# Layer 0 attention: the row maxima turned by VectorE and carried by DMA into a spare row of the queries, and the causal mask as four 32-row products per head

## The chip, the cores and the metric

The kernel runs on one core of one Trainium2 chip. The metric is device time in microseconds, the median of three runs. All times below are microseconds unless ns is written. The engines are named as in the profile: PE is TensorE, DVE is VectorE, ACT is ScalarE, POOL is GpSimd, SP is SyncE, which issues most DMAs.

## The reference, cut to what matters

The kernel computes two pre-norm transformer layers on x of 4 x 512 x 256. Layer 0 is a causal attention of 16 heads of 16, and a mixture of 8 experts; layer 1 is an attention over the four sequences at equal positions, and a gated MLP with 4-bit weights. The change lies in layer 0's attention:

```python
q, k, v = (qkv[0], qkv[1], qkv[2])
att = jnp.einsum('bhqd,bhkd->bhqk', q, k) / math.sqrt(HEAD_DIM)
causal = jnp.triu(jnp.ones((s, s), dtype=bool), k=1)
att = jnp.where(causal[None, None, :, :], jnp.float32(-1000000000.0), att)
att = jax.nn.softmax(att, axis=-1)
out = jnp.einsum('bhqk,bhkd->bhqd', att, v)
```

Layer 1's attention is touched in one operand only: a 0/1 pattern with which its scores are multiplied, so that each token sees only the four tokens of its own position.

## The kernel before

**Tiling.** The 512 positions are cut into four blocks j of 128. The 16 heads form four groups g of four; head h of a group lives in the partitions 32h to 32h+31. The tile `qk` (L463) holds, for each group, six slots of [4 sequences x 128 positions]: slots 0 to 3 are the keys of the four blocks, slots 4 and 5 the queries of the current block (slot 4 + j mod 2). A head's 32 partitions are used so: rows 4 to 19 hold the 16 dimensions, which `project` (L534) sends there by DMA from a staging tile, eight DMAs per half. Rows 0 to 3 of the keys hold a constant pattern, one in row g of group g, which POOL writes beforehand from `mask32` (`blank`, L470, and L481); rows 0 to 3 of the queries begin as zeros (L485, L506).

**Batches.** The attention runs in 44 batches n (L649): for every block j and sequence s, four, two, one or one groups at a time. A batch has five steps:

- `greatest` (L660): the scores, queries by keys, 16 x (groups / 4) matmuls on 32 rows each, into four PSUM tiles, one per head of the group. The pool `ps_sc` has five such banks.
- `mask` (L675): onto the last block of each tile, one bf16 matmul with the identity `ident_h` adds the upper triangle `later`, filled with -1e30. Then DVE takes the maximum over the keys, four TENSOR_REDUCEs at L687, into one of two tiles `maxes`.
- `shift` (L692): PE transposes `maxes` into PSUM (L697), so that each group's maxima stand in one of the rows 0 to 3 of the head's partitions; DVE subtracts the result from the queries (L700). The constant row of the keys then takes the maximum off all scores.
- `powers` (L706): the same scores a second time, keys by queries, so that keys lie on the partitions, now less the maximum (L716); ACT takes the exponential (L725), POOL zeroes what lies above the diagonal (L735).
- `mixed` (L743): the product with the values (L752), in the one bank of `ps_mm`, which the transposed maxima of `shift` use too.

**Order.** PE, DVE, POOL and ACT run in the order in which the program is written (`manual_schedule`, L73); SP does so too until batch 3 (L76, L899), and by priorities afterwards. The loop at L863 issues for batch n: `greatest(n + 1)`, `shift(n)`, `mask(n + 1)`, a filling, `mixed(n - 1)`, `powers(n)`, a second filling. A filling (`fill`, L149) takes pieces of the mixture of experts (L234, the router's and the experts' products, with the DVE work behind them), of projections of the next block and of layer norms, until a budget for PE or DVE is spent. The four routers' and experts' weight loads per batch (L891, n below 4) and the blanks of the later blocks (L893) follow.

**Start.** POOL first builds the identity, then copies and zeroes parts of `qk` (L481, L485), makes `ident_h` and `later`, and then computes two reciprocal roots for the first layer norm (L634). `blanks(xn)` (L500) zeroes `maxes` and the second query slot behind it.

**Elsewhere.** `mask8` (L95, L850) is `fold8` repeated four times; layer 1 multiplies by it at L1044.

## Time and profile before

| | us |
|---|---|
| median of three runs | 1166.89 (1166.68 to 1167.87) |
| span of the profiled execution | 1164.9 |
| PE busy | 1144.1 (98%) |
| DVE busy | 812.4 (70%) |
| ACT busy | 481.9 (41%) |
| POOL busy | 108.2 (9%) |

The profile is of one execution. Its span runs from the first to the last instruction; a run's time is some 2 more. The granted clock of TensorE is 0.999 on the mean. A group of instructions is shown as line, engine, operation, output <- input, shapes and count, then the busy time and the mean of one in ns, then the idle time of the engine before them and what ended it. An f32 matmul shows as two records, each with a weight load (PEld) of its own.

The lines that belong to the steps above, besides those that the prediction shows:

```profile
L716 PE MATMUL s<-qk 32*128 32x128 f32 x1280 | 54.5, 287 | 0.5
L697 PE MATMUL mxT<-ident,mx 128*128 128x128 f32 x44 | 14.4, 327 | 0.0
L681 PE MATMUL s<-later,ident_h 128*128 128x128 bf16 x128 | 12.4, 219 | 0.0
L700 DVE TENSOR_TENSOR qk<-qk,mxT 128x128 f32<-128x128 f32 x32 | 9.0, 282 | 15.0 <-PE mxT L697 14.9
L476 POOL COPY qk<-mask 128x512 f32<-128x512 f32 x12 | 7.5, 644 | 0.0
```

Durations of PE records overlap: a record of 219 ns starts 55 ns behind the one before it. What a piece adds to the time is read from the chain of waits in order of time, where each piece begins when the one before it ends.

Layer 0's attention takes the stretch from about 22 to 385. Busy time in parts of it:

| stretch | length | PE | DVE | ACT | POOL |
|---|---|---|---|---|---|
| 62 to 120 | 58.0 | 56.99 | 38.54 | 26.21 | 15.08 |
| 120 to 168 | 48.0 | 47.99 | 42.73 | 26.51 | 11.97 |
| 198 to 242 | 44.0 | 44.00 | 39.90 | 26.11 | 9.51 |
| 242 to 283 | 41.0 | 40.80 | 39.98 | 23.44 | 7.22 |
| 283 to 325 | 42.0 | 41.83 | 36.80 | 26.10 | 5.97 |
| 325 to 362 | 37.0 | 35.85 | 34.74 | 20.80 | 4.55 |

### The profile page before, as it was taken

The page shows a single profiled execution, that of the slowest core. Times are in us where ns is not written, and L with a number is a line of the kernel's source. Part 1 is how long each engine was busy: PE and PEld are TensorE (multiplying, and loading weights), DVE is VectorE, ACT ScalarE, POOL GpSimd, SP SyncE. Part 2 cuts the span into 40 slices and gives each one's busy share as a digit, 9 for nine tenths or more (in the row PEclk, how much of TensorE's full clock was granted, in tenths as well). Part 3 has the DMA queues.
Part 4 walks back from the last instruction along what each step waited for, and adds up shares of the span by engine and source line. Part 5 has one row for each costly group of instructions (what it writes and reads, how often), then busy time and mean ns, then how long its engine had stood idle before and what let it go on. Part 6 is the DMA issues. An engine that isn't in the chain of part 4 may idle for free.

```text
span 1164.9 us, 18575 instructions
## 1 busy us (share of the span) xinstructions
PE 1144.1 (98%) x7182; PEld 662.6 (57%) x7182; DVE 812.4 (70%) x1788; ACT 481.9 (41%) x1095; POOL 108.2 (9%) x153
## 2 busy tenths in 40 slices
PE   9999999999998999999999999999999999999998
PEld 5666555555554445555555555566544475484487
DVE  6675899999988844868663776687699835716710
ACT  1444555555655542444443444444344313303300
POOL 8322221212112000000000000000000000000000
PEclk9999999999999999999999999999999999999999
DMA  4440100000000500000000001110110000000000
GB/s 130 118 120 2 27 12 1 2 2 2 2 2 1 181 1 1 1 1 0 1 1 1 1 1 46 33 51 19 27 46 1 0 1 19 0 1 19 1 19 18
DMA packets 21527, 26.46 MB, mean 23 GB/s; under 512 B 5160, under 2 KB 15144, under 8 KB 21440
## 3 DMA queue, kind: packets, MB, share of 16 engines
q1 hardware_dynamic: 20624, 24.10, 7.6%
q10 hardware_dynamic: 816, 1.18, 0.4%
q8 instruction: 56, 0.92, 0.3%
q14 instruction: 31, 0.25, 0.1%
HBM read 18.97 MB, written 2.10 MB: 18 GB/s over the span
## 4 chain that ended last, share of the span: by engine, by line
PE 82%; DVE 13%; issue 2%; ACT 1%; POOL 1%; SPq 0%; DMA 0%; POOLq 0%; DVEq 0%; ACTq 0%
PE qk_ps L1019 11%; PE y L1266 9%; PE o L1110 9%; PE g L948 9%; PE u L948 9%; PE lg_ps L234 8%; PE eo L234 7%; PE s L668 3%; PE s L716 3%; DVE mx L687 3%; PE av L752 2%; PE v_ps L1001 2%; PE qk_ps L539 2%; PE a L1090 1%; PE s L1032 1%
## 5 line engine op out<-in xcount | busy, mean ns | idle before, releaser
L1019 PE MATMUL qk_ps<-xT,wqkv 128*128 128x512 f32 x320 | 148.9, 599 | 2.3 <-ACT part L323 1.2
L234 PE MATMUL lg_ps<-rw,xT 128*128 128x512 f32 x256 | 122.5, 601 | 1.4 <-ACT xT L986 0.3
L234 PE MATMUL eo<-ew,xT 128*128 128x512 f32 x256 | 121.5, 600 | 0.8 <-ACT lg L297 0.5
L1110 PE MATMUL o<-wpj,oT 128*128 128x256 f32 x512 | 119.1, 382 | 0.0
L1266 PE MATMUL y<-wd,it 128*128 128x256 f32 x512 | 111.8, 379 | 0.0
L1110 PEld LDWEIGHTS o<-wpj,oT 128*128 128x128 f32 x512 | 95.9, 190 | 27.5 <-issue 14.3
L1266 PEld LDWEIGHTS y<-wd,it 128*128 128x128 f32 x512 | 97.0, 190 | 15.0 <-issue 2.2
L687 DVE TENSOR_REDUCE mx<-s 128x1 f32<-128x384 f32 (+3 forms) x176 | 100.5, 633 | 0.2 <-PE s L681 0.2
L1019 PEld LDWEIGHTS qk_ps<-xT,wqkv 128*128 128x128 f32 x320 | 59.1, 190 | 71.4 <-issue 57.4
L725 ACT ACTIVATE pt<-s 128x512 f32<-128x512 f32 (+1 forms) x176 | 84.1, 565 | 35.9 <-PE s L716 35.9
L948 PE MATMUL g<-xT,wgu 128*128 128x512 f32 x192 | 90.4, 593 | 0.0
L948 PE MATMUL u<-xT,wgu 128*128 128x512 f32 x192 | 90.2, 592 | 0.0
L323 ACT ACTIVATE part<-eo,c 128x256 f32<-128x256 f32 x128 | 53.6, 471 | 84.7 <-PE eo L234 74.8
L735 POOL TENSOR_SCALAR_AFFINE_SELECT pt<-pt 128x256 f32<-128x256 f32 (+2 forms) x88 | 62.4, 716 | 246.9 <-ACT pt L725 246.7
L1244 ACT ACTIVATE th<-sq 128x512 f32<-128x512 f32 x64 | 40.3, 630 | 87.8 <-DVE sq L1243 87.8
L234 PEld LDWEIGHTS lg_ps<-rw,xT 128*128 128x128 f32 x256 | 46.1, 190 | 46.1 <-issue 37.3
L234 PEld LDWEIGHTS eo<-ew,xT 128*128 128x128 f32 x256 | 46.1, 190 | 45.7 <-issue 38.3
L222 DVE TENSOR_TENSOR xres<-xres,y 128x256 f32<-128x256 f32 x16 | 6.7, 421 | 92.5 <-PE y L1266 92.5
L297 ACT COPY lg<-lg_ps 128x512 f32<-128x512 f32 x64 | 37.6, 588 | 73.5 <-PE lg_ps L234 73.5
L185 POOL TENSOR_TENSOR ln_rs<-rs_v,minus_half 128x4 f32<-128x4 f32 x15 | 16.6, 1103 | 552.2 <-DVE rs_v L184 440.0
L1245 DVE SCALAR_TENSOR_TENSOR th<-th,g 128x512 f32<-128x512 f32 x63 | 43.2, 686 | 29.3 <-ACT th L1244 29.2
L948 PEld LDWEIGHTS u<-xT,wgu 128*128 128x128 f32 x192 | 36.5, 190 | 45.9 <-issue 44.7
(240 smaller groups left out, 1782.5 us busy)
## 6 DMA issues: line engine op xcount, KB each, us to landing
qk<-stage SPq DMA_DIRECT2D x56, 64.0 KB, 2.4
wqkv<-in_w_qkv SPq DMA_DIRECT2D x8, 320.0 KB, 6.4
rw<-in_router_w SPq DMA_DIRECT2D x8, 256.0 KB, 4.8
ew<-in_expert_w SPq DMA_DIRECT2D x8, 256.0 KB, 5.5
wpj<-in_w_proj SPq DMA_DIRECT2D x1, 2048.0 KB, 12.5
out<-xres SPq DMA_DIRECT2D x4, 512.0 KB, 2.7
xres<-in_x SPq DMA_DIRECT2D x3, 512.0 KB, 4.8
dq_wgu<-in_gate_w SPq DMA_DIRECT2D x8, 128.0 KB, 2.4
```

Source lines behind the costliest of these rows:

```text
L234: nc.tensor.matmul(ps, lhsT=xT[:, hc, (g % 4) * P : (g % 4 + 1) * P], rhs=w[:, hc, 2 * pair : 2 * pair + 2, :].rearrange("p e o -> p (e o) ...
L297: nc.scalar.copy(lg[:, 2 * pair : 2 * pair + 2, :].rearrange("p e o -> p (e o)"), ps)
L323: nc.scalar.mul(part[:, e % 4], ps[:, i], c[:, e : e + 1])
L687: nc.vector.tensor_reduce(maxes[n % 2][:, h, gs[0] : gs[0] + nb], ps[:, : nb * nk].rearrange("p (b k) -> p b k", b=nb), AX.X, ALU.max,)
L725: nc.scalar.activation(pt[:, i, : nb * nk], tiles[2 * pair + i][:, : nb * nk], AF.Exp, scale=0.25)
L735: nc.gpsimd.affine_select(out=last, in_=last, compare_op=ALU.is_ge, fill=0.0, base=0, pattern=pattern, channel_multiplier=-1,)
L948: nc.tensor.matmul(ps, lhsT=wgu[:, w, half, jj, par * P : (par + 1) * P], rhs=xT[:, half, :], start=half == 0, stop=half == 1,)
L1019: nc.tensor.matmul(ps, lhsT=wqkv[:, hc, kv, h, :], rhs=xT[:, hc, :], start=hc == 0, stop=hc == 1,)
L1110: nc.tensor.matmul(ys[t // 2][:, t % 2], lhsT=state["o"][:, h, t * P : (t + 1) * P], rhs=wpj[:, HPK * kv + h, :], start=kv == 0 and h == 0 ...
L1244: nc.scalar.activation(th, sq, AF.Tanh, scale=0.7978845608028654)
L1245: nc.vector.scalar_tensor_tensor(th, th, 1.0, gp, ALU.add, ALU.mult)
L1266: nc.tensor.matmul(ps, lhsT=it[:, c // 2, c % 2, t * P : (t + 1) * P], rhs=wd[:, c // 2, c % 2, :], start=c == 0, stop=c == 2 * NJ - 1,)
```

## The change

The 16 dimensions of a head now stand in rows 0 to 15 of its 32 partitions, and row 16 is a spare row. In the keys it holds -1, which four DMAs write at the start from a tile `minus`; in the queries it takes the maximum of each query. The first scores use rows 0 to 15, the second rows 0 to 16.

The maxima are laid down in one tile [128 queries, group, 32], heads in the first four columns. DVE turns them in blocks of 32 x 32 (`mT`, one buffer), so that partition 32a + h holds head h's maxima of the queries 32a to 32a+31. Four DMAs from SP, one for each a, write them into row 16 of the four heads. PE's transpose, its place in `ps_mm` and DVE's subtraction go.

`shift(n + 1)` now follows `mask(n + 1)`, where `shift(n)` stood between `greatest(n + 1)` and `mask(n + 1)`; `shift(0)` is issued before the loop.

The mask's one product of 128 rows per tile becomes four of 32 rows. The rows c of a diagonal block, 32 queries at a time, have their own triangle in the columns from 32c on; `pick` chooses the 32 output rows, and head h's product reads the partitions 32h to 32h+31. The loop over c is outside, that over the heads inside.

The pattern rows of the keys, the zeroed queries, `ident_h` and `mask8` are not needed any more; layer 1 multiplies by `fold8` with another view of the same elements. POOL's blanks of later blocks shrink to those of the values, and the conditions that waited for the others go.

```diff
     fold8 = const.tile([P, 8], F32, name="fold8")
-    mask8 = const.tile([P, NS, 8], F32, name="mask8")
...
         qk = w0.tile([P, 4, NBLK + 2, NS, P], F32, name="qk")
-        maxes = [w0.tile([P, 4, 32], F32, name=f"mx{i}") for i in range(2)]
+        maxes = w0.tile([P, 4, 32], F32, name="mx")
+        nc.vector.memset(maxes, 0.0)
         va = w0.tile([P, NBLK * NS * NH0 * 17 + 15], F32, name="va")
...
         wo = w0.tile([P, 2, HID], F32, name="wo")
-        def blank(j, i):
-            if i == 4:
-                to = va.shape[1] if j == NBLK - 1 else (j + 1) * per_block
-                nc.gpsimd.memset(va[:, j * per_block : to], 1.0)
-            else:
-                nc.gpsimd.tensor_copy(
-                    qk[:, i, j].rearrange("p s q -> p (s q)"),
-                    mask32[:, i : i + 1].to_broadcast([P, 512]),
-                )
-        nc.gpsimd.tensor_copy(
-            qk[:, :, 0].rearrange("p g s q -> p g (s q)"),
-            mask32[:, :4].unsqueeze(2).to_broadcast([P, 4, 512]),
-        )
-        nc.gpsimd.memset(qk[:, :, NBLK].rearrange("p g s q -> p g (s q)"), 0.0)
-        ident_h = w0.tile([P, P], BF16, name="ident_h")
-        nc.gpsimd.tensor_copy(ident_h, ident)
+        def blank(j):
+            to = va.shape[1] if j == NBLK - 1 else (j + 1) * per_block
+            nc.gpsimd.memset(va[:, j * per_block : to], 1.0)
+        minus = b1.tile([P, HID], F32, tag="w1", name="minus")
+        nc.gpsimd.memset(minus, -1.0)
+        for g in range(4):
+            nc.sync.dma_start(
+                out=qk[16:P:32, g, :NBLK].rearrange("p j s q -> p (j s q)").rearrange(
+                    "p (i k) -> p i k", k=HID
+                ),
+                in_=minus[0:4].unsqueeze(1).to_broadcast([4, 8, HID]),
+            )
+        pick = w0.tile([P, 224], BF16, name="pick")
+        nc.gpsimd.memset(pick, 0.0)
+        nc.gpsimd.tensor_copy(pick[:, 96:P], mask32)
         later = w0.tile([P, P], BF16, name="later")
         nc.gpsimd.memset(later, 0.0)
-        nc.gpsimd.affine_select(
-            out=later, in_=later, compare_op=ALU.is_ge, fill=NEG,
-            base=0, pattern=[[-1, P]], channel_multiplier=1,
-        )
+        for i in range(4):
+            nc.gpsimd.affine_select(
+                out=later[32 * i : 32 * i + 32], in_=later[32 * i : 32 * i + 32],
+                compare_op=ALU.is_ge, fill=NEG, base=0, pattern=[[-1, P]], channel_multiplier=1,
+            )
         bs = b1.tile([P, 2, 512], F32, tag="hi4", name="bs")
...
         bp = rows[:, 8:].rearrange("p i q -> p (i q)")
-        def blanks(xn):
-            after = b2.tile([P, 1], F32, tag="rs_v", name="after")
-            nc.gpsimd.tensor_copy(after, xn[:, 3, 0:1])
-            for i in range(2):
-                nc.gpsimd.memset(maxes[i], 0.0)
-            nc.gpsimd.memset(qk[:, :, NBLK + 1].rearrange("p g s q -> p g (s q)"), 0.0)
         def split_biases():
...
                     eng.dma_start(
-                        out=qk[h + 4 : h + 20, 2 * half + r // 4, j : to + 1 : to - j].rearrange(
+                        out=qk[h : h + 16, 2 * half + r // 4, j : to + 1 : to - j].rearrange(
                             "p i s q -> p i (s q)"
...
                 for s in (0, 2):
-                    yield need("PE", 1.75, 1, cond=lambda: blanked > 5 * j - 10)
+                    yield need("PE", 1.75, 1, cond=lambda: blanked > j - 2)
                     values(j, xT, s)
...
                         "PE", 1.75, 0 if half or i else 1,
-                        cond=lambda: j < 2 or done >= 8 * j - 12 and blanked >= 5 * j - 5,
+                        cond=lambda: j < 2 or done >= 8 * j - 12,
                     )
...
                 for h in range(4):
-                    r = slice(32 * h, 32 * h + 32)
+                    r = slice(32 * h, 32 * h + 16)
                     nc.tensor.matmul(
...
                         lhsT=queries(j, g)[r, s], rhs=qk[r, g, : j + 1, s, :],
...
             j, s, gs = batches[n]
...
             tiles = open_scores.pop(n)
-            for ps in tiles:
-                nc.tensor.matmul(
-                    ps[:, : nb * nk].rearrange("p (b k) -> p b k", b=nb)[:, :, j * P :],
-                    lhsT=ident_h, rhs=later.unsqueeze(1).to_broadcast([P, nb, P]),
-                    start=False, stop=True,
-                )
+            for c in range(4):
+                for h, ps in enumerate(tiles):
+                    r = slice(32 * h, 32 * h + 32)
+                    left_of = P - 32 * c
+                    nc.tensor.matmul(
+                        ps[:, : nb * nk].rearrange("p (b k) -> p b k", b=nb)[
+                            :, :, j * P + 32 * c :
+                        ],
+                        lhsT=pick[r, 96 - 32 * c : 224 - 32 * c],
+                        rhs=later[r, :left_of].unsqueeze(1).to_broadcast([32, nb, left_of]),
+                        start=False, stop=c == 3,
+                    )
             for h, ps in enumerate(tiles):
                 nc.vector.tensor_reduce(
-                    maxes[n % 2][:, h, gs[0] : gs[0] + nb],
+                    maxes[:, :nb, h],
                     ps[:, : nb * nk].rearrange("p (b k) -> p b k", b=nb), AX.X, ALU.max,
...
         def shift(n):
             j, s, gs = batches[n]
-            ps = ps_mm.tile([P, P], F32, tag="mm", name=f"mxT_{n}")
-            nc.tensor.transpose(ps, maxes[n % 2].rearrange("p h g -> p (h g)"), ident)
             g, nb = gs[0], len(gs)
-            q = qk[:, g : g + nb, 4 + j % 2, s, :]
-            nc.vector.tensor_tensor(
-                q, q, ps.unsqueeze(1).to_broadcast([P, nb, P]), ALU.subtract
-            )
+            mT = a1.tile([P, 4, 32], F32, tag="mT", name=f"mT_{n}")
+            nc.vector.transpose(
+                mT[:, :nb].rearrange("p b q -> p (b q)"),
+                maxes[:, :nb].rearrange("p b h -> p (b h)"),
+            )
+            for a in range(4):
+                nc.sync.dma_start(
+                    out=qk[16:P:32, g : g + nb, 4 + j % 2, s, 32 * a : 32 * a + 32],
+                    in_=mT[32 * a : 32 * a + 4, :nb],
+                )
         powers_of = {}
...
                     for h in range(4):
-                        r = slice(32 * h, 32 * h + 32)
+                        r = slice(32 * h, 32 * h + 17)
                         nc.tensor.matmul(
...
                             lhsT=qk[r, g, c, s, :], rhs=queries(j, g)[r, s],
...
         xn = normed_by_twos()
-        blanks(xn)
         xT = a1.tile([P, 2, NS, P], F32, tag="xT0", name="xT0_0")
...
         normed.clear()
-        for i in range(5):
-            blank(1, i)
+        blank(1)
         split_biases()
...
         )
-        nc.vector.tensor_copy(mask8, fold8.unsqueeze(1).to_broadcast([P, NS, 8]))
         xT = unused("xT0_1", "p (h s q) -> p h s q", h=2, s=NS)
...
         greatest(0)
         mask(0)
+        shift(0)
         inputs = {1: Stream(projections(1, xT))}
...
                 if n + 1 < NBT:
                     greatest(n + 1)
-                shift(n)
                 if n + 1 < NBT:
                     mask(n + 1)
+                    shift(n + 1)
             fill(PE=(2.0, 2.0, 1.8, 1.6)[j], DVE=2.6)
...
                     loaded[n // 2, (4 * n % 8 + i) // 2] = slot
-            for _ in range(1 + (n < 2) if blanked < 10 else 0):
-                blank(2 + blanked // 5, (blanked + 4) % 5)
+            if blanked < 2:
+                blank(2 + blanked)
                 blanked += 1
...
         ps_y = l1.enter_context(tc.tile_pool(name="l1_y", bufs=1, space=PSUM))
-        seen = mask8.rearrange("p s b -> p (s b)").unsqueeze(1).to_broadcast([P, 16, 32])
+        seen = fold8.unsqueeze(1).to_broadcast([P, 64, 8])
         state = {}
...
             )
-            nc.vector.tensor_tensor(sm, sm, seen, ALU.mult)
+            by_8 = sm.rearrange("p i (s b) -> p (i s) b", b=8)
+            nc.vector.tensor_tensor(by_8, by_8, seen, ALU.mult)
             sc = c1.tile([P, 16, 4], F32, tag="sc", name=f"sc{p}")
...
                 sc.rearrange("p i s -> p (i s)"),
-                sm.rearrange("p i (s b) -> p (i s) b", b=8), AX.X, ALU.add,
+                by_8, AX.X, ALU.add,
             )
```

## The prediction

> **What bounds the kernel now.** I read the page's chain of waits first, then the same chain in order of time inside layer 0, then the timeline there, and last the groups of instructions and the DMA issues. All numbers are microseconds unless marked ns.

> ```profile
> PE 82%; DVE 13%; issue 2%; ACT 1%; POOL 1%; SPq 0%; DMA 0%; POOLq 0%; DVEq 0%; ACTq 0%
> PE qk_ps L1019 11%; PE y L1266 9%; PE o L1110 9%; PE g L948 9%; PE u L948 9%; PE lg_ps L234 8%; PE eo L234 7%; PE s L668 3%; PE s L716 3%; DVE mx L687 3%; PE av L752 2%; PE v_ps L1001 2%; PE qk_ps L539 2%; PE a L1090 1%; PE s L1032 1%
> ```

> TensorE sets the end; the change touches only lines worth a few per cent each, and VectorE (DVE) is the one rival. The chain in order of time shows one batch bounded by TensorE:

> ```profile
> 203.26 0.86 PE s L668 x8
> 204.12 0.26 PE mxT L697
> 204.38 0.22 PE s L681 x4
> 204.60 1.77 PE eo L234 x4
> 206.38 0.79 PE av L752 x24
> 207.17 0.88 PE s L716 x24
> 208.05 1.91 PE eo L234 x4
> ```

> Columns: start, length, what. First scores, transpose of the maxima, mask, filler, mixing, second scores, filler. The same four records of filler cost 1.77 behind the mask, which uses the whole array, and 1.91 behind the second scores, which use 32-row quarters: leaving quarters costs 0.14. In j=3 (four blocks of keys) some batches are bounded by DVE instead:

> ```profile
> 249.61 0.20 DVE qk L700
> 249.81 2.40 DVE mx L687 x4
> 252.20 0.08 DVE sums L436
> ```

> Summed over 24 to 365, DVE holds about a quarter of the chain. I count 13 of the 44 batches as DVE-bound, all of one head group; 31 as TensorE-bound: 19 of one group (j=2, 3), 8 of two (j=1), 4 of four (j=0).

> **TensorE: mask and transpose.** Gone for a batch of one, two, four groups are the transpose, 0.26, and the mask, 0.22, 0.44, 0.86 (four products of 128 columns per group, so 0.055 per 128 columns in bf16). Added are 16 products on 32 rows. No row has bf16 products on 32 rows. The nearest are L716 and L668: L716 takes 0.88 for 24 records (above) and 1.10 for 32 (j=3), so 8 records of 128 f32 columns add 0.22, that is 0.11 for each four. A full-array f32 record of 512 columns takes 0.43 (1.72 over four), so 128 columns 0.107: the four quarters run wholly beside each other. In that case a head's columns alone count, 128+96+64+32 = 320 per group, and 320 at 0.055 per 128 is 0.14, 0.28, 0.55. Then the filler follows quarters and not the whole array: +0.14. Per batch: 0.14+0.14-0.26-0.22 = -0.20; 0.28+0.14-0.26-0.44 = -0.28; 0.55+0.14-0.26-0.86 = -0.43. The other bound is that the quarters run one after another: 1280 columns, 0.55, 1.10, 2.20, which makes +0.21, +0.54, +1.22. I take the first, since L716 and L668 have the same rows, banks and order. That the maxima fall due a little later (all four tiles close together at the end of the mask) is met by the transpose that no longer stands ahead of it.

> The trace's own starts inside one four of L716 lie 6.6 ns apart (275.649, 275.656, 275.663, 275.669). [...]

> On the path I count 19 x 0.20 = 3.8, of which I keep three quarters, 2.9, because DVE is busy 39.9 of 44.0 in 198 to 242 and 36.8 of 42.0 in 283 to 325 and will take back some; 7 x 0.28 = 2.0 (one batch of j=1 lies beside the wait for layer norm at 81 to 92); 3 x 0.43 = 1.3 (batch 0's mask ends in a wait for DVE). Together -6.2; from -10.4 (all 44 in full) to +13.2 (31 batches, one after another).

> **VectorE.** Gone are 44 subtractions L700, 0.28, 0.42, 0.69 busy and 0.20 on the chain; added are 44 transposes of 32, 64, 128 columns.

> ```profile
> L687 DVE TENSOR_REDUCE mx<-s 128x1 f32<-128x512 f32 x64 | 39.6, 681 | 0.0
> L687 DVE TENSOR_REDUCE mx<-s 128x1 f32<-128x384 f32 x64 | 31.1, 548 | 0.0
> L1041 DVE STREAM_TRANSPOSE sm<-s 128x512 f32<-128x512 f32 x16 | 11.4, 715 | 28.1 <-PE s L1032 28.1
> ```

> 128 columns are worth 133 ns between the first two; 480 columns fewer than L1041 leave 715 - 499 = 216 ns. So 0.20 goes and 0.2 comes: 0 in the 13 DVE-bound batches, between -0.1 and +0.2 each (-1.3 to +2.6). In the TensorE-bound ones DVE's idle tenth hides it; without that cover it would cost the same 0.2. The transpose waits in addition until the four DMAs of the batch before have read `mT` (one buffer); behind it stand DVE's filler and the next four maxima, for which the second scores wait (five banks). Layer 1's multiplication by `fold8` instead of `mask8` keeps 128x512 elements; L1044 and L1070 take 692 ns each with either operand, so 0. L850 (1.41 at 22.1) falls away beside TensorE's scores: 0.

> **SyncE and the new wait.** Four DMAs per batch are new, 176 in all, and the second scores wait for them where they waited for L700. Behind those scores in TensorE's order stand the filler and the next mixing, and ACT's exponentials wait for them. The nearest rows:

> ```profile
> qk<-stage SPq DMA_DIRECT2D x56, 64.0 KB, 2.4
> dq_sgu<-in_gate_s SPq DMA_DIRECT2D x64, 16.0 KB, 1.7
> 33.20 5.61 SPq L549 DMA_DIRECT2D qk<-stage  x8
> 242.35 2.48 DVE L687 TENSOR_REDUCE mx<-s 128x1 f32<-128x512 f32 x4
> 251.26 1.55 PE L716 MATMUL s<-qk 32*128 32x128 f32 x32
> ```

> Three issues of L549 go before the fourth starts: 3 x 0.64; with the transpose, 0.2, the fourth's issue and landing, 2.4, and a handing over or two, about 4.6 to 5.2. The batch shown (28) has its maxima at 244.83 and its scores at 251.26: 6.4 of room, because `shift` is moved ahead by a whole step, past one filling, a mixing and another batch's scores. Read so for all 44, the room is 5.1 at batch 0, 5.6 at the next smallest, 7.5 at the median. `mT` comes free likewise: the maxima of neighbours end 6.1 or more apart but for batch 1 (4.0). I take +0.5 for batches 0 and 1. In SP's queue the move passes stage DMAs (eight per half, 5.1) and the router and expert loads. The stage sets of j=2 start at 67.9 and 76.5, of j=3 at 134.2 and 141.7; the maxima of batches 5 and 6 end at 67.7 and 76.25, of 13 and 14 at 134.3 and 141.3, so each set would come just behind a shift and be done before the next one: 0, and up to 2 each if the order is the other way.

> **Start and GpSimd.** Up to the first root POOL loses these copies and gains small memsets and three selects of 0.29:

> ```profile
> 1.92 1.88 POOL qk L481
> 3.80 1.74 POOL qk L485
> 6.28 1.50 POOL ln_rs L634 x2
> ```

> About 4.4 of POOL work becomes some 2.3, so the roots wait for their variances alone (5.57 and 6.53; statistics that run beside POOL's copies take 0.78 where others take 0.39). The second root would end at 7.3 or earlier instead of 7.78: -0.7, between 0 and -1.5. The four DMAs of `minus` put 1.7 ahead of the second load of x, which is used only at 10.67: 0. Later blanks (12 x 0.64 and a memset of 1.8) lie on an engine busy 9%: 0.

> **Sum.** -6.2 + 0 + 0.5 - 0.7 = -6.4, against the profiled execution's span of 1164.9: 1158.5. The median of the runs is 1166.89, 2.0 more than that span; with the same 2.0, 1160.5. I say 1161.

> **Rivals.** (1) The DMAs come late, slower. For: eight stage DMAs on the two queues have landed after 3.8, the longest issue took 1.44. Against: the rooms above. It decides where transpose, issues and landing exceed 6.7: summed over the batches' rooms, that is 7.0 of delay, which eats the gain. At 7.2 it is 14.3, so 1166.9 - 6.4 + 14.3 = 1174.8; 0.17. (2) The quarters' bf16 products run one after another: +13.2 + 0.5 - 0.7, 1180; halfway to it, 1170. Against it is L716; 0.11. (3) No change: 16 weight loads per batch set the mask's pace (L681's load takes 0.098; four rounds are 0.39, so +0.05, -0.17, -0.43 per batch), or DVE takes back all of the rest: some 1165.5; 0.19. What speaks for it is DVE's nine tenths.

> **How the numbers follow.** Faster 0.53, these rivals 0.17, 0.11 and 0.19. From -10.4 the low end is 1156; the high end reaches into (1) and (2) to 1172, with some 0.12 above and 0.07 below. The forecast's own range is 1156 to 1164.5. About 0.2%, 2.3, is what a measurement of this kernel can tell from no change: faster 0.53, within it 0.19, slower 0.28.

> **What would show it.** In the chain of the changed kernel, no mxT; L681's successor at 0.14 to 0.2 for one group; the filler behind it at 1.91; transposes of about 0.22 with no wait for a DMA; second scores waiting for maxima and not for DMAs; the second root done by 7.3. It is wrong if the mask of one group takes 0.4 or more, if waits of TensorE or DVE for a `qk<-mT` DMA add up to over 5, or if DVE's part of the chain grows by what TensorE's loses.

## The result, and the profile after

The changed kernel took 1174.74 us (four runs, 1173.9 to 1177.43), the kernel before, run beside it, 1167.06: ratio 1.007, 95% interval 1.0056 to 1.0085. It is slower, by some 8 us, and outside the range that was forecast. The profiled execution's span is 1172.6 against 1164.9.

The page's parts on busy time, on the granted clock in 40 slices, and on the chain of waits:

```profile
PE 1148.4 (98%) x7666; PEld 668.7 (57%) x7666; DVE 808.4 (69%) x1788; ACT 481.2 (41%) x1095; POOL 96.0 (8%) x140
...
PEclk8999997999999999999999999999999999999999
...
PE 81%; DVE 13%; ACT 1%; issue 1%; DMA 1%; SPq 1%; POOL 0%; DVEq 0%; POOLq 0%; ACTq 0%
```

TensorE still sets the end and DVE's part of the chain has not grown. New in the chain are SP's queue and a DMA, 1% each. TensorE is busy 4.3 longer than before, although it has less to do; the clock line, 9 in every slice before, shows an 8 and a 7.

One batch in layer 0, the chain in order of time (start, length, what), as for the kernel before:

```profile
212.90 0.86 PE s L660 x8
213.76 0.14 PE s L676 x15
213.90 1.91 PE eo L233 x4
215.82 0.79 PE av L753 x24
216.61 0.88 PE s L717 x24
```

Here the change does what was forecast. Scores, mask and filler took 0.86 + 0.26 + 0.22 + 1.77 = 3.11 and take 0.86 + 0.14 + 1.91 = 2.91. Where the clock stays full, the second scores of neighbouring batches come 0.20 closer together in j=2 (batches 12 to 15: 6.22, 6.02, 5.82, 5.61 behind the same scores of the kernel before) and 0.26 closer in j=1 (batches 2 to 6, between whose second scores stand the masks of batches 4 to 7: 6.56 down to 5.54).

But the attention begins late. The chain in order of time at the start:

```profile
3.78 0.68 SPq L478
4.46 0.04 issue
4.50 1.57 SPq L478
6.07 0.04 issue
6.12 7.06 DMA xres<-in_x
13.17 0.02 issue
13.20 0.44 DVE ln_st L179
...
16.82 3.15 DVE xn L193 x4
19.97 0.60 DVE stage L535
20.57 0.04 issue
20.62 6.29 PE v_ps L553 x16
```

SP's four DMAs of -1 (L478) hold up the second load of x; the layer norm of block 1 waits for it, DVE comes late to a copy that `v_ps` of block 0 needs, and `v_ps` then takes 6.29 where it took 3.72. The first scores begin at 28.27 instead of 22.43. TensorE's timeline of the kernel before, then the first scores of the changed kernel (start, length, line, output <- input, count):

```profile
17.34 3.72 PE L561 MATMUL v_ps<-wp,xT 128*128 128x256 f32 x16 [0.60 <-DVE stage L543]
22.43 2.08 PE L668 MATMUL s<-qk 32*128 32x128 f32 x32
```

```profile
28.27 1.17 PE L660 MATMUL s<-qk 16*128 16x128 f32 x32
```

And the gain does not last. Busy time in stretches of the changed kernel, then of the kernel before (stretch, its length, busy time and count of PE, PEld, DVE, ACT, POOL, then the granted clock, DMA's share, GB/s):

```profile
20.00:40.00 20.00, 18.30 (x161) 12.49 (x161) 9.62 (x17) 1.17 (x2) 8.40 (x16) 0.77 0.24 54
160.00:200.00 40.00, 39.13 (x405) 21.95 (x405) 34.67 (x89) 20.15 (x57) 8.92 (x11) 0.87 0.03 5
240.00:270.00 30.00, 30.00 (x342) 15.60 (x344) 28.28 (x67) 17.68 (x51) 5.30 (x8) 0.94 0.01 1
```

```profile
20.00:40.00 20.00, 19.42 (x199) 13.26 (x202) 12.26 (x21) 4.22 (x8) 11.92 (x20) 1.00 0.38 74
160.00:200.00 40.00, 38.59 (x387) 21.11 (x390) 37.75 (x96) 22.33 (x62) 9.19 (x12) 1.00 0.01 1
240.00:270.00 30.00, 29.80 (x325) 16.94 (x324) 27.94 (x61) 16.66 (x47) 4.13 (x6) 1.00 0.01 1
```

The trace's record of the granted clock says where: it halves at 19.0, 32.7, 97.5, 176.0, 196.5, 257.9 and 353.5, for 3.41 or 6.83 each time, 34.1 in all. Two of these stretches (columns as above):

```profile
19.01:25.83 6.82, 5.21 (x12) 4.21 (x13) 2.84 (x6) 0.00 (x0) 6.39 (x8) 0.50 0.40 68
176.02:182.85 6.83, 6.83 (x56) 4.01 (x54) 5.60 (x17) 3.11 (x7) 0.93 (x2) 0.50 0.02 3
```

In the kernel before the clock never halves between 6 and 1150. Batch 16 stands 5.54 behind the kernel before, batch 20 10.85 behind. That is where the gain went.

So there were two suspects, the DMAs of -1 at the start and the clock. The clock needed a reason: the change takes full-array work away (the transpose, the 128-row mask) and runs the scores on 16 and 17 rows of each quarter instead of 32.

### The profile page after: what moved, and what is told of

The parts are those of the page before. It is cut to its first block, busy times and chain, and to the rows that moved or that the text cites. A ratio compares the mean times of both kernels' runs of the same rounds, so it can differ in the third digit from the quotient of the medians.

```text
span 1172.6 us, 19877 instructions
## 1 busy us (share of the span) xinstructions
PE 1148.4 (98%) x7666; PEld 668.7 (57%) x7666; DVE 808.4 (69%) x1788; ACT 481.2 (41%) x1095; POOL 96.0 (8%) x140
## 4 chain that ended last, share of the span: by engine, by line
PE 81%; DVE 13%; ACT 1%; issue 1%; DMA 1%; SPq 1%; POOL 0%; DVEq 0%; POOLq 0%; ACTq 0%
PE qk_ps L1018 11%; PE y L1266 9%; PE o L1110 9%; PE g L947 9%; PE lg_ps L233 9%; PE u L947 9%; PE eo L233 7%; DVE mx L685 3%; PE s L717 3%; PE s L660 3%; PE av L753 2%; PE v_ps L1000 2%; PE a L1090 1%; PE s L1031 1%; PE qk_ps L531 1%
## 5 line engine op out<-in xcount | busy, mean ns | idle before, releaser
L233 PE MATMUL lg_ps<-rw,xT 128*128 128x512 f32 x256 | 127.7, 623 | 1.6 <-ACT aT L791 0.4
L233 PE MATMUL eo<-ew,xT 128*128 128x512 f32 x256 | 125.0, 614 | 0.8 <-ACT lg L296 0.5
L1110 PE MATMUL o<-wpj,oT 128*128 128x256 f32 x512 | 119.1, 382 | 0.0
L1266 PE MATMUL y<-wd,it 128*128 128x256 f32 x512 | 111.8, 379 | 0.0
L1110 PEld LDWEIGHTS o<-wpj,oT 128*128 128x128 f32 x512 | 95.9, 190 | 27.5 <-issue 14.3
L1266 PEld LDWEIGHTS y<-wd,it 128*128 128x128 f32 x512 | 97.0, 190 | 15.0 <-issue 2.2
L221 DVE TENSOR_TENSOR xres<-xres,y 128x256 f32<-128x256 f32 x16 | 6.7, 421 | 92.2 <-PE y L1266 92.2
```

The source lines that it names most:

```text
L233: nc.tensor.matmul(ps, lhsT=xT[:, hc, (g % 4) * P : (g % 4 + 1) * P], rhs=w[:, hc, 2 * pair : 2 * pair + 2, :].rearrange("p e o -> p (e o) ...
L1110: nc.tensor.matmul(ys[t // 2][:, t % 2], lhsT=state["o"][:, h, t * P : (t + 1) * P], rhs=wpj[:, HPK * kv + h, :], start=kv == 0 and h == 0 ...
L1266: nc.tensor.matmul(ps, lhsT=it[:, c // 2, c % 2, t * P : (t + 1) * P], rhs=wd[:, c // 2, c % 2, :], start=c == 0, stop=c == 2 * NJ - 1,)
```

## The experiments

The kernel before was run beside each; its median lay between 1166.37 and 1166.54. "Stretches" are those at half clock between 13 and 395 in the profiled run; a run's mean clock tells how many it had (34.1 at half clock go with the 0.985 of the changed kernel's profiled run).

**late_ones.** The changed kernel with only the DMAs of -1 moved.

```diff
-        for g in range(4):
-            nc.sync.dma_start(out=qk[16:P:32, g, :NBLK]..., in_=minus[0:4]...)
...
         load_x(1)
         nc.sync.dma_start(out=wo, in_=w_out.rearrange("(k p) o -> p k o", p=P))
+        for g in range(4):
+            nc.sync.dma_start(out=qk[16:P:32, g, :NBLK]..., in_=minus[0:4]...)
```

> The changed kernel with its four DMAs of -1 moved behind the second load of x and the load of w_out on SP; nothing else. Theory 'start': in the changed kernel these DMAs hold SP for 3.9 (2.2 to 6.1), the second load of x lands at 13.2, TensorE stands idle 16.2 to 20.6 and the granted clock then falls to a half for 6.8, so that the first scores begin at 28.3 instead of 22.4. It expects v_ps to begin at about 16.5, the first scores at 21.5 to 22.5, no half clock before 25, and 5 to 7 less than the changed kernel: 1168 to 1169.5. Rival 'the other parts': the start is caught up later, or the DMAs only move their cost, then less than 2 is won: above 1172.5.

1170.4 (ten runs, 1165.41 to 1171.93), ratio 1.0019 [1.0005, 1.0033], 4.3 less than the changed kernel, a little less than expected. `v_ps` starts at 17.41 and takes 3.72; the first scores start at 22.50, as before the change. The half clock begins at 25.7, and six stretches, 34.1 in all, remain. The start was one cause, the clock is another.

**after_32_rows and after_16_rows.** The changed kernel with both scores on all 32 rows; the unused rows have to be zeroed, by POOL, and the -1 is written block by block. Its control has the same zeroing and DMAs with 16 and 17 rows.

```diff
+            nc.gpsimd.memset(qk[:, :, j].rearrange("p g s q -> p g (s q)"), 0.0)
+            ones(j)
...
-                    r = slice(32 * h, 32 * h + 16)
+                    r = slice(32 * h, 32 * h + 32)
...
-                        r = slice(32 * h, 32 * h + 17)
+                        r = slice(32 * h, 32 * h + 32)
```

> The changed kernel with both scores on all 32 rows of a head (rows 17 to 31 zeroed by GpSimd as the kernel before did, the -1 written per block behind w_out). The first scores then meet the maxima of two blocks earlier in row 16, so the maxima are those of shifted scores; the softmax is the same. Theory 'rows': TensorE's clock is granted by how many rows of the array work, and products on 16 and 17 of 128 rows count half of what products on 32 rows count; the changed kernel has seven spells of half clock (34.1 in all), each after a stretch of 3.4 in which rows x columns x time filled 0.34 or less of the array. It expects no spell between 40 and 385, a clock of 0.998 or more, and 6 to 10 less than its control on 16 and 17 rows: 1158 to 1162. Rival 'waits': the spells come from TensorE's waits alone; then spells, clock (0.985 to 0.99) and time are those of the control within 2.

> The control of the run on 32 rows: the same zeroing by GpSimd and the same DMAs of -1 per block, but the scores on 16 and 17 rows as in the changed kernel. Theory 'rows': four to six spells of half clock between 30 and 385, clock 0.986 to 0.991, 1167 to 1170. Rival 'waits': the same time and clock as the run on 32 rows.

1173.24 (ratio 1.0052 [1.0036, 1.0068]) and 1177.85 (1.01 [1.0075, 1.0125]), both above what was expected. As a cure after_32_rows missed: its POOL work stands ahead of the first layer norm, so that `qk_ps` begins at 12.02 instead of 9.60 and takes 8.83 instead of 7.13, with half clock from 12.5, and batch 2 is already 10.0 late. Between batches 4 and 43 it gains 1.3 on the kernel before. Against its control, which differs in rows alone, it is 4.6 faster: the rows count. Neither has the good start, so a pair that has it follows below.

**before_20_rows.** The kernel before, with rows 20 to 31 of each quarter, which hold zeros, left out of both scores.

```diff
-                    r = slice(32 * h, 32 * h + 32)
+                    r = slice(32 * h, 32 * h + 20)
...
-                        r = slice(32 * h, 32 * h + 32)
+                        r = slice(32 * h, 32 * h + 20)
```

> The kernel before with both scores on rows 0 to 19 of a head instead of 0 to 31; rows 20 to 31 are zeros, so the values are the same. Theory 'rows': by the same measure, counted over the trace of the kernel before with 20 rows, none to two stretches of 3.4 fall to 0.34 or below, depending on where the stretches lie: none to two spells, clock 0.996 to 0.999, 0 to +4 (1167 to 1171). Rival 'waits': no spell, clock 0.999, within 1 of the kernel before.

1169.64 (1167.96 to 1172.03), ratio 1.0026 [1.0014, 1.0037]. Nothing else in the program differs, no instruction is added or removed, and two stretches at half clock appear, of 10.2 at 24.5 and 3.4 at 253.2. Leaving out rows that hold zeros made the kernel slower, 1169.64 against 1166.41. Not all of it shows in the mean clock: three of its seven runs have 0.998 or 0.999 and still took 1167.96 to 1168.51; what cost these 1.6 to 2.1 is not shown.

**turned_32_rows, both_32_rows, turned_16_rows, both_16_rows.** Four kernels with the start of the kernel before (the -1 of the keys comes from POOL copies where the 0/1 pattern was written) and the transposed maxima of the change: with the mask of before or in quarters, on 32 or on 16 and 17 rows (the diffs of these two are those of after_full_mask and after_32_rows). The -1, against the changed kernel:

```diff
+    key4 = const.tile([P, 4], F32, name="key4")
+    nc.vector.tensor_scalar(key4, mask32[:, 16:17].to_broadcast([P, 4]), -1.0, None, ALU.mult)
...
-            nc.sync.dma_start(out=qk[16:P:32, g, :NBLK]..., in_=minus[0:4]...)
+                nc.gpsimd.tensor_copy(
+                    qk[:, i, j].rearrange("p s q -> p (s q)"),
+                    key4[:, i : i + 1].to_broadcast([P, 512]),
+                )
```

> The part of the change that turns the maxima on VectorE and writes them by four DMAs, alone: the mask as before on the whole array, both scores on all 32 rows, and the keys' -1 written by GpSimd's copies where the 0/1 column of before was written, so that no DMA of -1 stands ahead of the second load of x. Row 16 of the queries holds the maxima of two blocks before while the first scores run: a constant per query, which the softmax takes out again. Theory (start and clock): the start is that of before within 1 us at the second scores of batch 0, no or one stretch of 3.4 us at half clock between 20 and 360, and the transpose gone from TensorE gives 0.2 to 0.27 per TensorE-bound batch: 1159 to 1163. Rival (waits for DMAs and VectorE's transposes are the loss): 1168 to 1175, with the granted clock as before.

> As turned_32_rows, with the mask in four 32-row products per head as in the change. Theory (start and clock; the mask's own cost as predicted): within 2 us of turned_32_rows, 1158 to 1164, or up to 5 more if the full-array mask that is gone lets stretches at half clock appear. Rival (the quarters run one after another): 8 to 13 above turned_32_rows with the clock unchanged, and a mask of one group longer than 0.5 us.

> turned_32_rows with one thing changed: the first scores on 16 rows of each quarter and the second on 17, as in the change. Every instruction, transfer and wait is the same otherwise. Theory (TensorE's share of rows at work sets the granted clock): stretches of 3.4 to 6.8 us at half clock appear between 20 and 360 where turned_32_rows had two, and the time rises to 1164 to 1170. Rival (the clock follows idle time or instructions only): within 1 us of turned_32_rows, 1160.5 to 1162.5.

> both_32_rows with the first scores on 16 rows and the second on 17. It has both parts of the change and the fewer rows, and no DMA of -1 ahead of the second load of x. Theory: 1167 to 1172, four to seven stretches at half clock, like the changed kernel with its DMAs of -1 moved (1170.4). Rival: as both_32_rows, 1163 to 1166.5.

| | mask as before | mask in quarters |
|---|---|---|
| 32 rows | 1161.50 (1161.35 to 1163.03), clock 0.997 to 1.000 | 1165.76 (1162.83 to 1166.49), 0.994 to 0.999 |
| 16 and 17 rows | 1166.78 (1163.96 to 1169.11), 0.988 to 0.994 | 1172.49 (1171.53 to 1173.14), 0.983 to 0.984 |

The ratios are 0.9958 [0.9941, 0.9974], 0.999 [0.998, 0.9999], 0.9998 [0.9989, 1.0008] and 1.0049 [1.0034, 1.0064]. Each of these steps, which take rows from the array, cost time and clock: the rows 5.3 and 6.7, the mask 4.3 and 5.7. The rival that the clock follows instructions or idle time alone expected turned_16_rows at 1162.5 at most. One way from the kernel before to the changed one is 1166.4, less 4.9 for the transposed maxima, plus 4.3 for the quarters, plus 6.7 for the rows, plus 2.3 from both_16_rows to the changed kernel, 1174.8. These are differences of neighbouring medians, so their sum must come out; what they tell is the sizes, and those depend on the order. Why the last step is smaller than late_ones' 4.3 is not shown. Both late_ones and both_16_rows have a stretch of 6.8 at the start, at 25.7 and 27.2; they differ in their setup, and both_16_rows has one stretch that is 3.4 longer, at 170.6.

**after_full_mask.** The changed kernel with the 128-row mask of before.

```diff
-            for c in range(4):
-                for h, ps in enumerate(tiles):
-                    r = slice(32 * h, 32 * h + 32)
...
+            for ps in tiles:
+                nc.tensor.matmul(
+                    ps[:, : nb * nk].rearrange("p (b k) -> p b k", b=nb)[:, :, j * P :],
+                    lhsT=ident_h, rhs=later.unsqueeze(1).to_broadcast([P, nb, P]),
+                    start=False, stop=True,
+                )
```

> The changed kernel with the mask on the whole array as before, all else as changed. Theory (start and clock): the start stays as in the changed kernel, 5 to 6 us late at the first scores; full-array work in the thin windows may take one or two of the later stretches at half clock away: 1169 to 1175. Rival (the quartered mask is the loss): 1158 to 1164.

1170.03 (ten runs, 1167.05 to 1176.21), ratio 1.0032 [1.0016, 1.0048]: 4.7 less than the changed kernel, with the late start and 30.7 at half clock in the profiled run. The quartered mask is part of the loss, not the whole, and not by its own length, which is 0.14 for 0.22 in the chain shown above.

**before_quarters_2.** The kernel before with the quartered mask alone; its constants are set up behind the blanks.

```diff
-            for ps in tiles:
-                nc.tensor.matmul(
...
+            for c in range(4):
+                for h, ps in enumerate(tiles):
+                    r = slice(32 * h, 32 * h + 32)
```

> The kernel before with the mask in four 32-row products per head, alone (the set-up of the mask's constants behind the blanks; layer 1 multiplies by fold8). By the predicted sizes of the mask alone next to nothing: 1165 to 1168 with the full clock; since both_32_rows stood 4.3 above turned_32_rows at 0.995, by the clock theory up to two stretches at half clock, to 1172. Rival (the quarters run one after another): 1174 to 1180 with the full clock and a mask of one group over 0.5 us.

1173.6 (1173.33 to 1173.73), ratio 1.0059 [1.0042, 1.0075], clock 0.997: neither of the two. The chain in order of time in j=2:

```profile
208.62 0.86 PE s L662 x8
209.48 0.26 PE mxT L697
209.74 0.26 PE s L678 x16
210.00 1.91 PE eo L233 x4
```

The four quarters do run beside each other (one after another they would take the 0.55 that the prediction estimates), but behind a product that used the whole array they take 0.26 and not 0.14, and the filler behind them 1.91 and not 1.77. So the mask alone is worth +0.18 per batch of one group (3.29 against 3.11), where "next to nothing" was expected; from batch 0 to 43 that adds up to 3.0. The other 3.8 is lost by batch 0, around one stretch of 6.8 at half clock at 28.1; at the granted clock of 0.50 such a stretch costs at most half its length, an estimated 3.4, and the rest is not assigned. Read beside turned_32_rows (0.86 + 0.33 + 1.77 = 2.96, so -0.15), the two parts alone would make +0.03, and together they make -0.20: without the transpose the mask follows the scores' quarters directly, and a change between quarters and the whole array, 0.11 to 0.14 in these chains (0.33 for 0.22, 0.26 for 0.14, 1.91 for 1.77), comes only once.

**after_warm and after_warm_5.** The changed kernel with products on the whole array put where TensorE waits for `v_ps`; nothing reads them. First ten products, then five.

```diff
                 if half == (not j) and j < 2:
+                    if not j:
+                        ps = ps_mm.tile([P, 4, P], F32, tag="mm", name="warm")
+                        for i in range(5):
+                            nc.tensor.matmul(
+                                ps, lhsT=ident, rhs=ident.unsqueeze(1).to_broadcast([P, 4, P]),
+                                start=not i, stop=i == 4,
+                            )
```

> The changed kernel with ten products of 512 columns on the whole array put into TensorE's idle 4.45 us ahead of v_ps of block 0; nothing reads what they compute. Theory (the idle time at the start makes TensorE pay a second time, by a half-clock stretch): v_ps 3.7 instead of 6.28 us, the second scores of batch 0 some 2.5 us earlier, no half clock between 19 and 26, 1171 to 1173.5 (the later stretches stay). Rival (v_ps was slow for another reason, as reading late operands): v_ps still about 6.3, the time as of the changed kernel or up to 1 us longer.

> The changed kernel with five products of 512 columns on the whole array ahead of v_ps of block 0: ten records of 0.43, 4.3 us, as long as TensorE's idle time there (4.45). Nothing reads what they compute. Theory: v_ps 3.6 instead of 6.28, no half clock from 19 to 26, the first scores at 25.7 instead of 28.3; the later stretches stay and may move: 1171 to 1174 against 1174.7. Rival: v_ps still 6.3, the time 1174 to 1175.

1175.52 (1.0077 [1.0055, 1.0099]) and 1174.33 (1.0067 [1.0051, 1.0083]). A product of 512 f32 columns is two records of 0.43, so ten took 8.75, twice the idle time. With five, PE's timeline (start, length, line, output <- input, count):

```profile
16.32 4.46 PE L602 MATMUL warm<-ident 128*128 128x512 f32 x10
20.61 3.62 PE L553 MATMUL v_ps<-wp,xT 128*128 128x256 f32 x16
24.06 0.60 PE L209 MATMUL x_ps<-ident,xn 128*128 128x128 f32 x4
25.01 0.66 PE L209 MATMUL x_ps<-ident,xn 128*128 128x128 f32 x4 [0.35 <-DVE va L559]
25.60 1.35 PE L667 MATMUL s<-qk 16*128 16x128 f32 x28
```

`v_ps` is back at 3.62 with its operands as late as ever, and the first scores start at 25.60, 2.7 earlier: the half clock alone had made `v_ps` long, 6.29, of which the first 5.2 ran at 0.50. Yet the median is only 0.4 lower, which lies within the spread of the runs and where the rival had it. The next thin stretch now brings 6.8 at half clock at 29.9, and batch 0's second scores gain 0.3. A cure in one place moved the loss.

**both_16_filled, both_32_filled.** both_16_rows and both_32_rows with two such products at each of eight places where the trace shows TensorE waiting or on few rows: 32 records, 13.8 of work.

```diff
             with tc.high_priority(offset=AHEAD):
+                if n + 1 in (1, 8, 18, 21, 25, 29, 38):
+                    ps = ps_mm.tile([P, 4, P], F32, tag="mm", name=f"fill_{n}")
+                    for i in range(2):
+                        nc.tensor.matmul(
+                            ps, lhsT=ident, rhs=ident.unsqueeze(1).to_broadcast([P, 4, P]),
+                            start=not i, stop=i == 1,
+                        )
                 if n + 1 < NBT:
                     greatest(n + 1)
```

The eighth place is ahead of `mixed(39)`.

> both_16_rows with work added: ahead of the first scores of batches 1, 8, 18, 21, 25, 29, 38 and ahead of the mixing of batch 39, two products of 512 f32 columns on the whole array each (four records of 0.43, 1.72 us; 13.8 us over the eight places), into a bank that nothing reads. Theory (too little of the array at work halves the clock): the stretches of 34 us at half clock go to two at most, clock 0.995 or more, and the time falls though work is added: 1162 to 1168 against 1172.5. Rival (the narrow products themselves lower the clock): the stretches stay, and the time rises by what of the 13.8 is not idle, to 1174 to 1184.

> both_32_rows with the same eight places filled. Theory: the stretches that nine of its ten runs had more of than the profiled one go, clock 0.998 or more in all runs; the filling costs up to 4 where TensorE did not wait: 1159 to 1164, with a spread under 1. Rival: 1168 to 1178, as the added work costs its length.

1161.21 (1160.98 to 1163.17), ratio 0.9954 [0.9936, 0.9972], and 1162.22 (1162.12 to 1162.77), 0.9964 [0.9949, 0.9979]. 13.8 of useless work makes both_16_rows 11.3 faster. Its narrow products are all still there, so they do not lower the clock by themselves: it was 0.998 to 1.000 in the four runs with the work added, against 0.983 and 0.984 without. Busy time in two stretches of both_16_rows and of both_16_filled (columns as above):

```profile
160.00:200.00 40.00, 39.22 (x398) 22.31 (x402) 34.21 (x91) 20.01 (x57) 8.80 (x11) 0.80 0.01 2
240.00:270.00 30.00, 30.00 (x352) 16.53 (x342) 28.22 (x69) 17.18 (x49) 4.15 (x8) 0.94 0.01 1
```

```profile
160.00:200.00 40.00, 38.77 (x476) 21.45 (x472) 38.02 (x97) 22.63 (x64) 9.04 (x11) 1.00 0.01 2
240.00:270.00 30.00, 29.77 (x382) 17.39 (x378) 28.69 (x62) 17.34 (x50) 4.18 (x8) 1.00 0.01 2
```

The clock goes from 0.80 to 1.00 in the first, 78 more matmul records, 8 of them added ones, fit into the same 40 us, and PE's busy time falls. both_32_filled had the full clock in all five runs and a spread of 0.7; filling is not free where the clock would have held: ahead of `mixed(39)` its lead on the kernel before falls by 1.3, from 2.8 to 1.5. But by batch 43 the lead is 3.5 again, so this does not account for its median, which is 0.7 above that of turned_32_rows; what does is not shown.

**after_mended.** The changed kernel itself with two edits, whose diffs are shown above: that of late_ones and the eight fillings.

> The changed kernel, whole, with the four DMAs of -1 behind the second load of x and wo, as in late_ones, and the eight places filled as in both_16_filled. Theory (the early DMAs and the clock are the whole loss, the change's own steps cost what was predicted): 1160 to 1163, clock 0.996 or more. Rival (the DMAs of the maxima, or SP's queue, cost something of their own that the clock hid): 1164 to 1170 with a clock of 0.995 or more.

1161.99 (1161.2 to 1162.96), ratio 0.9955 [0.9938, 0.9973], clock 0.998 to 1.000. With the two causes removed the changed kernel lies in the forecast's own range, 1156 to 1164.5. With both_16_filled (1161.2) and turned_32_rows (1161.5) it is faster than both kernels; the three cannot be told apart. turned_32_rows has nothing added and is the one to keep.

## Why the prediction was wrong, point by point

- **Where it failed first: "The four DMAs of `minus` put 1.7 ahead of the second load of x, which is used only at 10.67: 0."** SP's timeline of the changed kernel, and of the kernel before:

```profile
2.19 3.88 SPq L478 DMA_DIRECT2D qk<-minus  x4
6.12 0.97 SPq L61 DMA_DIRECT2D xres<-in_x  x1
```

```profile
2.19 0.43 SPq L61 DMA_DIRECT2D xres<-in_x  x1
```

  The four issues took 3.9, not 1.7 (the last one 1.57), and the load, once issued, took 7.06 to land where it had taken 5.7. In the kernel before it landed at 7.9, 2.8 ahead of its use at 10.67. That slack would have covered 1.7; it did not cover 3.9 and 1.4. The load landed at 13.17, 2.5 after 10.67, and DVE began with block 1's statistics at 13.20. TensorE's wait for it was priced nowhere. Undoing it alone gave 4.3.
- **Where it failed most: the sum holds no term for the clock.** Each row was taken from a profile at 0.999 and assumed to stay. The change takes 44 transposes and half the rows of the scores off the array in a kernel whose thinnest stretch of 3.41 had an estimated 0.35 of the array at work (by the count in the last section) and kept the clock at that 0.999. Neither the rivals nor the list of what would show the prediction wrong mentioned it. Giving the array work back in eight places was worth 11.3 in both_16_rows and 8.4 from late_ones to after_mended (1170.4 to 1162.0).
- **TensorE's price per batch was right where the clock was full**: -0.20 per one-group batch as forecast, -0.26 for -0.28 in j=1. That all of them add up to the -6.2 of the forecast is shown by no run: at the second scores of batch 43 after_mended stands 3.2 ahead of the kernel before and both_32_filled 3.5, with the cost of their filling in it. The mask of one group, 16 products on four different row groups, takes 0.14 in the chain, less than the 0.4 that would have shown the prediction wrong. The two parts of this step were sized wrongly one by one: the mask alone costs +0.18 and not +0.06, since quarters behind a full-array product take 0.26; the transpose makes up for it.
- **VectorE at 0 was right**: 808.4 busy against 812.4, the transposes 0.21 each in the chain where the subtraction was 0.20.
- **SyncE and the new wait, +0.5, was small as forecast**: in 20 to 390 the list of waits names one wait of DVE for a DMA of the maxima, of 0.2, and none of TensorE.
- **The roots come earlier as forecast, but their -0.7 reaches the attention in no run.** The second is done at 7.16 instead of 7.78 and `qk_ps` begins 0.57 earlier. In the changed kernel the late load hides that. In late_ones the load is in time, and still `v_ps` begins at 17.41 for 17.34. Block 1's normalization there starts 0.56 earlier and takes 0.63 longer (chain in order of time, kernel before, then late_ones):

```profile
14.17 2.52 DVE xn L194 x4
```

```profile
13.61 3.15 DVE xn L193 x4
```

  The first of these four takes 1.53 where it took 0.68. It now runs beside POOL's memsets of `va` and `rows` (1.00 and 0.52), which stood behind the blanks that the change removed; in the kernel before it runs beside copies of these blanks. In turned_32_rows and both_16_rows, where POOL makes such copies at that point, it takes 0.68 again.
- **The rivals.** The first one's 1174.8 is the time that was measured, by accident: its mechanism, DMAs of the maxima coming late, does not occur (the one wait of 0.2 above). The quarters do not run one after another (0.14 for one group where that was estimated at 0.55), and no change was not what happened.
- **The sum.** With the two causes removed again, after_mended took 1162.0 where 1161 was forecast. Against the kernel before run beside it that is 4.5 less, where 6.4 was forecast. Of the 1.9 between them 0.7 is the term of the roots; the rest is not assigned, and the cost of the filling is in it.

## What to carry to other kernels

Here four small DMAs put ahead of a load in its queue delayed it by their whole issue time, 3.9, so ask how late the load behind it may be, not when it is first used; and look for the small setup DMA that can go behind every load. On this kernel, in which TensorE is the bound, removing the full-array transposes saved 4.9 with the clock at 0.997 to 1.000, and using fewer rows cost 5.3 and 6.7 with the clock down to 0.983 to 0.994, so before taking work off the array find the thinnest few microseconds around each wait and count rows as well as time. If the mean granted clock drops by a percent after a change (0.985 for 0.999 here), compare at equal clock before blaming the change's own instructions, and test by adding work there.

## What the runs showed of the hardware that was not expected

```profile
193.09:196.50 3.41, 3.41 (x44) 2.28 (x42) 3.38 (x10) 2.10 (x7) 0.74 (x1) 1.00 0.02 5
254.53:257.94 3.41, 3.41 (x32) 1.97 (x27) 3.38 (x11) 2.54 (x8) 1.21 (x2) 1.00 0.01 1
350.10:353.51 3.41, 3.18 (x57) 2.32 (x50) 3.34 (x8) 0.92 (x4) 0.00 (x0) 1.00 0.00 0
```

By its records, whose ends are modelled, TensorE is busy in nearly all of each, mostly on 16, 17 and 32 rows, and the clock halves behind it, from 1.00 to 0.50. The changes of the clock keep to a grid: in the changed kernel's trace the half-clock stretches last 3.41 or 6.83, and the last six start 4, 23, 46, 52, 70 and 98 times 3.413 behind the first. To see what counts, I took each matmul record's length by its columns (0.43 per 512 f32 columns, half of that in bf16, as the mask's 0.055 per 128 has it), times its rows in use over 128, times its columns in use over 128, and summed this over windows of 3.41 in step with the half-clock stretches of the run, from 13 to 395. For the 14 traces with such a stretch (after_mended's is left out, for a test), 58 windows come right before a drop and 1421 do not:

| share of the window counted as | before a drop | no drop, smallest | best cut | windows on the wrong side |
|---|---|---|---|---|
| rows x columns in use | 0.12 to 0.39 | 0.35 | 0.37 | 6 of 1479 |
| a quarter in use counted as 32 rows | 0.12 to 0.57 | 0.36 | 0.405 | 31 |
| any product at work | 0.12 to 0.95 | 0.41 | 0.395 | 53 |

So in these traces the drop came after a window in which less than about 0.37 of the array's rows and columns were in use on the mean, with 6 of 1479 windows on the wrong side; the three windows shown have 0.20, 0.34 and 0.30. This is worked out from the records, some of which may be missing, and the cut was chosen on these same windows. The trace of after_mended tests it: its one drop comes behind a window of 0.35, and every other of its windows has 0.41 or more. That TensorE stands idle is not needed for a drop: in the first two windows shown it is busy for 3.41 of 3.41.

**The windows' phase seems to differ from run to run, and with it the time.** late_ones had runs at 1165.4 to 1167.1 (clock 0.990 to 0.992) and at 1170.4 to 1171.9 (0.984 and 0.985). That fits windows that fall differently over the same thin places, an estimate from the times and clocks that no trace shows. Between traces of different kernels the phase does differ: the first stretches of late_ones and turned_32_rows begin at 25.7 and 26.9. Of each kernel only one run was traced. By the count of rows and columns, a window of both_16_rows lies under about 0.37 wherever it starts in 22.0 to 26.8, 88.0 to 92.2, 166.9 to 171.2 or 190.0 to 193.9; these spans are longer than 3.41, so by this estimate every phase has a window there, and all four of its runs had 0.983 or 0.984. In the kernel before only starts in about 23.2 to 23.7 and 184.7 to 184.9 lie under it, 0.7 of 3.41, and none is far under it (0.35 at the least), so by the same estimate most phases miss both. Of its 63 runs beside the experiments two had a clock of 0.997 (1169.54 and 1169.69), all others 0.999 or 1.000: fewer than 0.7 of 3.41 would make, so windows this close to the cut mostly pass. The kernel was close to the edge before the change, which no row of its page shows. The phase itself was not set in any run.
